# Clipped score units with a second matmul, shared rows held in SBUF, and a table added by its own load

## The chip, the cores and the metric

The kernel runs on one core of one Trainium2 chip. The metric is the device time of one execution in microseconds (us), the median over several runs. The profile is one execution taken by the hardware profiler; its times are counted from the start of its span.

## The reference

One block of a transformer over x of shape (4, 2048, 256): an attention-like layer with a triangular ("bump") kernel in place of softmax, then a mixture of experts, each with a layer norm before and after and a residual. Cut to what matters here:

```python
# attention: B=4 batches, T=2048 tokens, H=16 heads, D=16 per head; per head one projected number per token
q_proj, k_proj = q @ Wproj.T, k @ Wproj.T            # (B, T, H)
bw = softplus(log_bandwidth) + 1e-4                  # (H,)
# out_i = sum_j max(0, 1 - |q_i - k_j| / bw_h) * v_j , divided by T
ctx = bump(q_proj, k_proj, v) / T
x = x + layernorm(ctx)
# experts: 64 experts, top 8, capacity 128 per expert, groups of 2 batches of the hidden states taken together
shared = silu(xn @ Wg) * (xn @ Wu) @ Wd * sigmoid(xn @ sgate)
y = sum over the 8 experts of weight_e * expert_e(xn)   # only the first 128 tokens of an expert count
x = x + layernorm(y + shared)
```

All arithmetic is fp32. The kernel computes the bump directly: with q and k already divided by the bandwidth and k negated, a score tile is min(|q - k|, 1) - 1, which is minus the triangle, and the sum over keys is a matrix product with v.

## The kernel before

**Score units.** A unit t is one batch b, one head h and one block s of 128 keys against all 2048 queries: a 128 x 2048 tile `hat` (keys on the partitions). There are 1024 units in a fixed order (`unit`): batch, group of 8 heads, parity p of the head, key block s, and innermost j = 0 to 3, the place of the head among four. 256 units make a batch (`NU`), 128 a group (`UG`). For each t the main loop writes out by hand `score(t)`, `evict(t)`, `product(t)`, and then one step of a background queue.

- `score(t)` normally has ACT compute |q + nk| into `hat` (line 1558) and DVE take min 1 and subtract 1 (line 1562). Now and then DVE makes the absolute value itself, in two more passes (lines 1553, 1555). A running number `spare` decides: it grows by 1.9 - 1.17 with each unit on ACT and falls by what DVE does besides and by 3.6 with each unit of the DVE kind; at 1.3 or more the next unit is of that kind.
- `product(t)` issues four matmuls on PE, one for each quarter c of 512 queries, staggered: quarter c of unit t - c. The stationary operand is the head pair's 128 x 32 value tile, and the output goes to rows 32j to 32j+31 of the PSUM bank `pa` for that quarter. So the four matmuls of a step lie in four different column groups of the array. A bank accumulates over the 128 units of a group.
- `evict(t)` scales a finished bank by -1/T into SBUF (line 1572).

Score tiles, the broadcast queries `qb` and some others come from 13 buffers of 128 x 2048 (`big`); `take` pops one while the program is written, `give` returns it. Ten smaller ones (`slot`) serve the background.

**Background.** The class `Background` holds tasks with an engine, a cost in us, dependencies and buffers. In each step of the main loop it emits, in queue order, the tasks that are ready by a table of lags (`LAG`), as long as the engine's debt is under its cap (`CAP`, per step: PE 0.84, from the third batch on 0.88). So all other work (projections of the next batches, the expert layer of finished ones, the experts over batches 0 and 1) is woven into the scoring at planned places, and each engine then runs its queue in order. What is left after the last unit is written out by `drain`, which plans without scoring.

**Expert results.** Rows of batches 0 and 1 go into one table `y_d[0]`; rows of batches 2 and 3 into two tables `y_d[1]`, `y_d[2]`. `finish(b)` computes the shared expert for the four 512-token chunks of a batch (`shared(c)`) and stores the rows as the start value of the table (line 619); for batch 2 (`NE` = 2) they are also stored to `ysh_d` (line 624), for a repair path that is normally skipped. The experts' results are then added by indirect accumulating DMAs from the POOL queue (line 1066 for the first half, line 1258 for the items of the second half). For the last batch the shared rows stay in SBUF, its table rows start from zeros (`zfill`), and the final norm adds them.

**Tail.** After the last unit: the last batch's front part, its routing (a chain of max and replace on DVE), the remaining shared rows, 15 items of hot experts, and `final(c)`, the last norm of each chunk: load the table rows from the SP queue (line 1281), for batches 2 and 3 a second table too and a DVE add (line 1288), add SBUF rows if there are any (line 1314), statistics (1292), scale with a power on POOL (1298), norm on ACT (1307), and an accumulating DMA from POOL onto the output (1321). The scatters of the items depend on `stored[2]`, the stores of batch 2's shared rows.

Of the kernel before, what the change touches and what calls it, by code (L numbers as in the profile page):

```python
# [25 lines left out]
class Background:  # L26
# [6 lines left out]
    CAP = {"pe": 0.84, "dve": 0.65, "act": 0.30, "pool": 1.5, "sp": 2.0}  # L33
# [107 lines left out]
def sandwich_kernel(ctx: ExitStack, tc: tile.TileContext, x_in, wqT, bq, wkT, bk, wvT, bv, wprojT, log_bw,  # L141
# [84 lines left out]
    with ExitStack() as ph:  # L226
# [29 lines left out]

        NES, ess = 4, []
# [11 lines left out]
        def give(tag):  # L269
            bg.free["big"].append((tag, bg.t))  # L270
# [12 lines left out]
        for t_ in vst:  # L283
            nc.gpsimd.memset(t_, 0.0)

# [170 lines left out]
        def finish(b, after=()):  # L456
# [104 lines left out]
            def shared(c):  # L561
# [56 lines left out]
                free_act = a  # L618
                free_ys = bg.add("sp", 1.0, lambda ys=ys, r0=r0: nc.sync.dma_start(yrows(r0, CH, 0),
# [647 lines left out]
        def final(env, c, deps, more=None, xd=(), tag=""):  # L1267
# [14 lines left out]
            l0 = l1 = bg.add("sp", 1.0, lambda: load(0), deps, get={yy: "big" if two else "slot"}, env=env)  # L1282
            if two:
                l1 = bg.add("sp", 1.0, lambda: load(1), [l0])
# [26 lines left out]
            if two:  # L1311
                a = bg.add("dve", 1.25, add, [a])
# [41 lines left out]
        lb = small.tile([P, H], F32, name="lb")  # L1354
# [26 lines left out]
        ab = small.tile([P, H], F32, name="ab")  # L1381
        nc.scalar.activation(ab, lb, AF.Abs)
        ex = small.tile([P, H], F32, name="ex")
        nc.scalar.activation(ex, ab, AF.Exp, scale=-1.0)
        u = small.tile([P, H], F32, name="u")
        nc.vector.tensor_scalar_add(u, ex, 1.0)
        lu = small.tile([P, H], F32, name="lu")
        nc.scalar.activation(lu, u, AF.Ln)
        one = small.tile([P, H], F32, name="one")
        nc.vector.tensor_scalar(one, u, 1.0, None, ALU.is_equal)  # L1390
        nc.vector.tensor_add(lu, lu, one)
        den = small.tile([P, H], F32, name="den")
# [149 lines left out]
        spare = [0.0]  # L1542

        def score(t):
# [7 lines left out]
            if spare[0] >= 1.3:  # L1552
                nc.vector.tensor_scalar(ht, qb[n][0], k, None, ALU.add)  # L1553
                hi = ht.bitcast(I32)
                nc.vector.tensor_scalar(hi, hi, 0x7fffffff, None, ALU.bitwise_and)  # L1555
                spare[0] -= 3.6
            else:
                nc.scalar.activation(ht, qb[n][0], AF.Abs, bias=k)  # L1558
                spare[0] += 1.9 - 1.17
            if s == NT - 1:  # L1560
                give(qb.pop(n)[1])
            nc.vector.tensor_scalar(ht, ht, 1.0, 1.0, ALU.min, ALU.subtract)  # L1562
# [16 lines left out]
        def product(t):  # L1579
            for c in range(4):  # L1580
# [5 lines left out]
                if w == 0:  # L1586
                    pa[k, c] = acc.tile([P, BK], F32, tag=f"pa{c}", name=f"pa_{k}_{c}")
                nc.tensor.matmul(pa[k, c][32 * j:32 * j + 32, :],  # L1588
                                 lhsT=vt[b, s].rearrange("p a w -> p (a w)")[:, h // 2 * VW + p * D:h // 2 * VW + p * D + 32],
# [200 lines left out]
```

## Time and profile before

| what | value |
|---|---|
| median of 3 runs | 2338.87 us (2335.26 to 2339.05) |
| profiled execution | 2339.91 us, span 2338.0 us |
| mean granted TensorE clock | 0.954 |
| PE, ACT, DVE busy | 1952.5, 1966.8, 1996.1 us |
| POOL busy | 490.4 us |
| first score unit done, last one done | 67.6 us, 2034.9 us |
| DMA moved | 274.32 MB, mean 117 GB/s |

In a row of the profile, a group of instructions is named by line, engine and operation, then what it writes and reads (out<-in, buffer numbers left out) with shapes and count; after the bar come the time it was busy, the mean of one in ns, and how long the engine had been idle just before, with what ended that idle time. PE is matrix multiplication, PEld its loading of weights, DVE the vector engine, ACT the scalar engine, POOL GpSimd, SP the engine that issues most DMAs. An fp32 matmul shows as two records.

### The profile page before, as it was taken

The numbers are of one execution on the slowest core, as the hardware profiler recorded it, in microseconds if no ns is written. First come the engines' busy times: TensorE is split into PE (matmuls) and PEld (weight loads), VectorE is DVE, ScalarE is ACT, GpSimd is POOL, SyncE is SP. The second block draws the span as 40 slices with busy tenths as digits, with TensorE's granted clock in tenths as the row PEclk, the third lists the DMA queues.
The fourth block names the chain that finished last, engine by engine and source line by source line (L and its number), as shares of the span: only waits on it lengthen the run. The fifth ranks groups of instructions, "written<-read, shape, count | busy, mean of one in ns | idle before, by whom it ended". The sixth has DMA issues, their size and how long they took to land. (4 is left out here: it accounts for less than half of the span.)

```text
span 2338.0 us, 32679 instructions
## 1 busy us (share of the span) xinstructions
PE 1952.5 (84%) x12552; PEld 687.2 (29%) x12552; DVE 1996.1 (85%) x3102; ACT 1966.8 (84%) x1269; POOL 490.4 (21%) x339
## 2 busy tenths in 40 slices
PE   7898979888799899677899887878888889987783
PEld 4332323222223222112222222223332223364342
DVE  4799999898999889999989998989999979886335
ACT  2899999898999998999999998989999989742213
POOL 1001010010120000003200003446553234442463
PEclk9999999999999999989999998999999999988897
DMA  4243534427351202142302014465544243355758
GB/s 127 91 133 120 184 103 153 151 88 264 117 162 64 91 19 70 37 147 69 112 19 81 28 54 122 114 186 151 174 121 136 57 134 90 102 177 147 177 124 197
DMA packets 195078, 274.32 MB, mean 117 GB/s; under 512 B 24833, under 2 KB 165505, under 8 KB 194145
## 3 DMA queue, kind: packets, MB, share of 16 engines
q1 hardware_dynamic: 165680, 235.33, 31.2%
q0 software_dynamic: 23824, 31.70, 8.3%
q10 hardware_dynamic: 5408, 5.11, 0.7%
q8 instruction: 101, 1.65, 0.3%
q14 instruction: 65, 0.52, 0.1%
HBM read 189.18 MB, written 82.90 MB: 116 GB/s over the span
## 5 line engine op out<-in xcount | busy, mean ns | idle before, releaser
L1558 ACT ACTIVATE hat<-qb,nk 128x2048 f32<-128x2048 f32 x959 | 1837.3, 1995 | 112.8 <-DMA qb<-zq_d 57.5
L1588 PE MATMUL pa<-hat,v 128*32 128x512 f32 x8192 | 1115.3, 620 | 284.4 <-DVE hat L1562 272.3
L1562 DVE TENSOR_SCALAR hat<-hat 128x2048 f32<-128x2048 f32 x1024 | 1230.3, 1223 | 97.2 <-ACT hat L1558 91.3
L1588 PEld LDWEIGHTS pa<-hat,v 128*32 128x32 f32 x8192 | 186.2, 110 | 900.0 <-DVE hat L1562 652.6
L1066 POOL DMA_INDIRECT y_d<-s,ix x64 | 147.8, 2309 | 286.7 <-DVE s L1064 145.4
L573 PE MATMUL k<-s,sgu 128*128 128x512 f32 x352 | 198.4, 651 | 0.0
L1041 POOL DMA_INDIRECT s<-tab_d,ix x64 | 106.0, 1657 | 327.6 <-DMA qb<-zq_d 259.0
L499 POOL TENSOR_TENSOR rsc<-rsc,mhalf 128x2 f32<-128x2 f32 x24 | 53.4, 2225 | 521.2 <-DVE rsc L498 521.0
L602 PE MATMUL k<-sd,s 128*128 128x256 f32 x384 | 113.7, 428 | 16.9 <-DVE s L589 7.4
L442 PE MATMUL k<-s,s 128*32 128x512 f32 x768 | 102.4, 592 | 0.0
L602 PEld LDWEIGHTS k<-sd,s 128*128 128x128 f32 x384 | 72.2, 205 | 86.4 <-issue 47.8
L573 PEld LDWEIGHTS k<-s,sgu 128*128 128x128 f32 x352 | 54.8, 192 | 136.3 <-issue 121.2
L305 POOL TENSOR_TENSOR rsa<-rsa,mhalf 128x4 f32<-128x4 f32 x16 | 30.8, 1925 | 290.9 <-DVE rsa L304 285.6
L1553 DVE TENSOR_SCALAR hat<-qb,nk 128x2048 f32<-128x2048 f32 x65 | 83.1, 1279 | 0.1
L1555 DVE TENSOR_SCALAR hat<-hat 128x2048 int32<-128x2048 int32 x65 | 79.9, 1229 | 2.2
L350 PE MATMUL k<-h,s 128*128 128x256 f32 x256 | 73.0, 413 | 0.0
L713 DVE MAX8 codes<-scT 128x8 f32<-128x1152 f32 (+2 forms) x48 | 63.4, 1321 | 0.2
L350 PEld LDWEIGHTS k<-h,s 128*128 128x128 f32 x256 | 45.4, 195 | 54.4 <-issue 48.6
L715 DVE MATCH_REPLACE8 scT<-codes,scT 128x1152 f32<-128x1152 f32 (+2 forms) x44 | 57.6, 1310 | 0.0
L607 DVE TENSOR_SCALAR s<-k,gt 128x256 f32<-128x256 f32 x48 | 22.8, 480 | 36.5 <-PE k L602 32.0
L442 PEld LDWEIGHTS k<-s,s 128*32 128x32 f32 x768 | 31.6, 138 | 54.0 <-issue 53.2
L1258 POOL DMA_INDIRECT y_d<-v,ix x28 | 39.9, 1426 | 23.5 <-DMA y_d<-s 7.9
(319 smaller groups left out, 1643.2 us busy)
## 6 DMA issues: line engine op xcount, KB each, us to landing
qb<-zq_d SPq DMA_DIRECT2D x128, 512.0 KB, 5.5
s<-m_d SPq DMA_DIRECT2D x48, 512.0 KB, 4.8
s<-_attn_hidden_states_dram SPq DMA_DIRECT2D x28, 512.0 KB, 5.5
v_d<-h SPq DMA_DIRECT2D x48, 192.0 KB, 2.6
v<-v_d SPq DMA_DIRECT2D x48, 192.0 KB, 2.5
h<-fn_expert_gate_up_w_dram SPq DMA_DIRECT2D x32, 256.0 KB, 3.5
s<-fn_expert_gate_up_w_dram SPq DMA_DIRECT2D x32, 256.0 KB, 2.8
b<-y_d SPq DMA_DIRECT2D x16, 512.0 KB, 9.3
```

The lines of the kernel that those rows point to most:

```text
L350: nc.tensor.matmul(env[pk][:, i * F:(i + 1) * F], lhsT=xv[:, k, o:o + P], rhs=wv[:, k, :], start=(k == 0), stop=(k == KF - 1))
L442: nc.tensor.matmul(env[pz][c * CR:(c + 1) * CR, :], lhsT=xv[:, r, :], rhs=env[mp][:, k * 2 * F:(k + 1) * 2 * F], start=(r == 0 and k == 0) ...
L573: nc.tensor.matmul(env[p_], lhsT=sgu[:, k, o:o + P], rhs=featview(env[xT])[:, k, :], start=(k == 0), stop=(k == KF - 1))
L602: nc.tensor.matmul(env[py][:, i * F:(i + 1) * F], lhsT=env[acts[f // 2]][:, o:o + P], rhs=sd[:, f, :], start=(f == 0), stop=(f == NI - 1))
L713: a = bg.add("dve", 1.25, lambda c8=c8: nc.vector.max(out=c8, in_=scT[:, :w]), ev + [a])
L1041: g = bg.add("pool", 1.3, lambda: nc.gpsimd.indirect_dma_start(out=xg(), out_offset=None, in_=tab_d[half][:, :], in_offset=bass.IndirectOf ...
L1066: s = bg.add("pool", 1.9, lambda: nc.gpsimd.indirect_dma_start(out=y_d[half][:, :], out_offset=bass.IndirectOffsetOnAxis(ap=iv(), axis=0), ...
L1553: nc.vector.tensor_scalar(ht, qb[n][0], k, None, ALU.add)
L1555: nc.vector.tensor_scalar(hi, hi, 0x7fffffff, None, ALU.bitwise_and)
L1558: nc.scalar.activation(ht, qb[n][0], AF.Abs, bias=k)
L1562: nc.vector.tensor_scalar(ht, ht, 1.0, 1.0, ALU.min, ALU.subtract)
L1588: nc.tensor.matmul(pa[k, c][32 * j:32 * j + 32, :], lhsT=vt[b, s].rearrange("p a w -> p (a w)")[:, h // 2 * VW + p * D:h // 2 * VW + p * D ...
```

## The change

Three things. (1) For a chosen unit, DVE makes two tiles: `hat`, q clipped between -nk and 1-nk, and `low`, q clipped between -1-nk and -nk. Their difference is min(|q + nk|, 1) up to a constant, so PE multiplies `hat` by v and `low` by -v (`neg`, made by DVE); the constant -1 becomes minus the sum of v over the keys, which POOL adds up in `pro` and PE and DVE turn into `csum`, subtracted at the eviction. The old DVE kind stays where buffers or the place in the group don't allow this one. (2) For chunks 2 and 3 of batch 2 the shared rows stay in SBUF and the final norm adds them; they are still stored to `ysh_d`, their table rows start from zeros, and they are no longer in `stored[2]`. (3) Where a chunk has rows in SBUF to add, its second table is loaded by an accumulating DMA from POOL onto the first, in place of a load and a DVE add. Beside these, the planner's PE caps become 0.86 and 0.92, the final norm's single load is planned with a delay of 9 steps, and scratch of the prologue is moved into one tile.

```diff
-    CAP = {"pe": 0.84, "dve": 0.65, "act": 0.30, "pool": 1.5, "sp": 2.0}
+    CAP = {"pe": .86, "dve": 0.65, "act": 0.30, "pool": 1.5, "sp": 2.0}
...
+        LATE, held = (2, 3), {}
...
+        pro = small.tile([P, 12 * D + 8], F32, name="pro")
+        near = const.tile([P, 3], F32, name="near")
+        csum = const.tile([P, 1], F32, name="csum")
+        for i in range(3):
+            nc.gpsimd.memset(near[:, i:i + 1], i - 1.0)
...
+                if b == NE and c in LATE:
+                    held[c] = env, ys, yy
+                    free_ys = bg.add("sp", 1.0, lambda ys=ys, c=c: nc.sync.dma_start(rows(ysh_d, c * CT, CH),
+                                                                                    chunkview(env[ys])), yy)
+                    return
...
-            l0 = l1 = bg.add("sp", 1.0, lambda: load(0), deps, get={yy: "big" if two else "slot"}, env=env)
-            if two:
+            l0 = l1 = bg.add("sp", 1.0, lambda: load(0), deps, get={yy: "big" if two else "slot"}, env=env,
+                             lat=None if two else 9)
+            onto = two and more is not None and not tag
+            if onto:
+                l1 = bg.add("pool", 1.3, lambda: nc.gpsimd.dma_start(y3(), yrows(r0, CH, 1), accum_op=ALU.add), [l0], lat=4)
+            elif two:
                 l1 = bg.add("sp", 1.0, lambda: load(1), [l0])
...
-            if two:
+            if two and not onto:
                 a = bg.add("dve", 1.25, add, [a])
...
+        def sums():
...
+            def mm():
+                for j in range(4):
+                    nc.tensor.matmul(env["cs"][2 * D * j:2 * D * j + 2 * D, :1], lhsT=pro[:, 2 * D * j:2 * D * j + 2 * D],
+                                     rhs=near[:, 2:3], start=True, stop=True)
+            q, bg.q = bg.q, []
+            a = bg.add("pe", 0.4, mm, get={"cs": "bank"}, env=env)
+            a = bg.add("dve", 0.15, lambda: nc.vector.tensor_copy(csum, env["cs"][:, :1]), [a], put=["cs"], env=env)
+            bg.q += q
+            bg.flush([a])
...
-            if spare[0] >= 1.3:
-                nc.vector.tensor_scalar(ht, qb[n][0], k, None, ALU.add)
...
+            u = t % NU
+            if u % UG == 0:
+                nc.gpsimd.memset(pro[:, :8 * D], 0.0)
+            room = 3 + (s >= 9) + (u % UG >= UG - 24)
+            if spare[0] >= 1.3 and 4 <= u % UG < UG - 12 and len(bg.free["big"]) >= room and (True):
+
+                low[t] = take(f"low_{b}_{h}_{s}")
+                i = len(clipped) % 2
+                kk = pro[:, 12 * D + 4 * i:12 * D + 4 * i + 3]
+                neg[t] = pro[:, (8 + 2 * i) * D:(10 + 2 * i) * D]
+                tot = pro[:, 2 * D * j:2 * D * j + 2 * D]
+                nc.vector.tensor_scalar(kk, near, k, None, ALU.subtract)
+                nc.vector.tensor_scalar(neg[t], value(t), -1.0, None, ALU.mult)
+                nc.gpsimd.tensor_tensor(out=tot, in0=tot, in1=value(t), op=ALU.add)
+                nc.vector.tensor_scalar(low[t][0], qb[n][0], kk[:, 0:1], kk[:, 1:2], ALU.max, ALU.min)
+                nc.vector.tensor_scalar(ht, qb[n][0], kk[:, 1:2], kk[:, 2:3], ALU.max, ALU.min)
+                clipped.add(t)
+                spare[0] -= 2.7
+                bg.debt["pe"] += 1.1
             else:
...
-                    nc.vector.tensor_scalar(ct[b, g][0][:, c * BK:(c + 1) * BK], pa.pop((k, c)), -1.0 / T, None,
-                                            ALU.mult)
+                    nc.vector.tensor_scalar(ct[b, g][0][:, c * BK:(c + 1) * BK], pa.pop((k, c)), csum, -1.0 / T,
+                                            ALU.subtract, ALU.mult)
...
+                if tt in low:
+                    nc.tensor.matmul(pa[k, c][32 * j:32 * j + 32, :], lhsT=neg[tt], rhs=low[tt][0][:, c * BK:(c + 1) * BK],
+                                     start=False, stop=False)
+                nc.tensor.matmul(pa[k, c][32 * j:32 * j + 32, :], lhsT=value(tt), rhs=hat[tt][0][:, c * BK:(c + 1) * BK],
+                                 start=first_, stop=last_)
...
+                if u % UG == UG - 8:
+                    sums()
...
-                    bg.CAP = dict(bg.CAP, pe=0.88, dve=0.75, act=0.4)
+                    bg.CAP = dict(bg.CAP, pe=.92, dve=0.75, act=0.4)
...
-                    if l < 0:
+                    if l < 0 and c - NE * NCH in held and not tag:
+                        e_, y_, d_ = held[c - NE * NCH]
+                        f_ = final(env, c, deps, lambda e_=e_, y_=y_: e_[y_][:, :CH * F], d_)
+                        bg.add("act", 0.0, lambda: None, [f_], put=[y_], env=e_)
+                    elif l < 0:
                         final(env, c, deps, tag=tag)
```

More of the change, by code (lines that the diff above doesn't have):

```diff
@@ L1350, in norm_x0 @@
             xt0.append(done)
-        lb = small.tile([P, H], F32, name="lb")
+        lb, ab, ex, u, lu, one, den = (pro[:, i * H:(i + 1) * H] for i in range(7))
         nc.sync.dma_start(lb, log_bw.rearrange("(a h) -> a h", a=1).to_broadcast([P, H]))
@@ L1378, in sandwich_kernel @@
         nc.sync.dma_start(bvb, bv.rearrange("(a f) -> a f", a=1).to_broadcast([P, F]))
-        ab = small.tile([P, H], F32, name="ab")
         nc.scalar.activation(ab, lb, AF.Abs)
-        ex = small.tile([P, H], F32, name="ex")
         nc.scalar.activation(ex, ab, AF.Exp, scale=-1.0)
-        u = small.tile([P, H], F32, name="u")
         nc.vector.tensor_scalar_add(u, ex, 1.0)
-        lu = small.tile([P, H], F32, name="lu")
         nc.scalar.activation(lu, u, AF.Ln)
-        one = small.tile([P, H], F32, name="one")
         nc.vector.tensor_scalar(one, u, 1.0, None, ALU.is_equal)
         nc.vector.tensor_add(lu, lu, one)
-        den = small.tile([P, H], F32, name="den")
         nc.vector.tensor_scalar_sub(den, u, 1.0)
@@ L1542, in sandwich_kernel, with value @@
         spare = [0.0]
+        low, neg, clipped = {}, {}, set()
+        def value(t):
+            b, g, p, s, j, h = unit(t)
+            o = h // 2 * VW + p * D
+            return vt[b, s].rearrange("p a w -> p (a w)")[:, o:o + 2 * D]
+        def sums():
+            env = {}
+            def mm():
[7 more added lines that the diff above has]
+            bg.flush([a])
         def score(t):
@@ L1551, in score @@
             k = nks[b][:, c:c + 1]
-            if spare[0] >= 1.3:
[L1553 to L1556, printed above, removed]
-            else:
-                nc.scalar.activation(ht, qb[n][0], AF.Abs, bias=k)
-                spare[0] += 1.9 - 1.17
+            u = t % NU
[16 more added lines that the diff above has]
+                bg.debt["pe"] += 1.1
+            else:
+                if spare[0] >= 1.3:
+                    nc.vector.tensor_scalar(ht, qb[n][0], k, None, ALU.add)
+                    hi = ht.bitcast(I32)
+                    nc.vector.tensor_scalar(hi, hi, 0x7fffffff, None, ALU.bitwise_and)
+                    spare[0] -= 3.6
+                else:
+                    nc.scalar.activation(ht, qb[n][0], AF.Abs, bias=k)
+                    spare[0] += 1.9 - 1.17
+                nc.vector.tensor_scalar(ht, ht, 1.0, 1.0, ALU.min, ALU.subtract)
             if s == NT - 1:
                 give(qb.pop(n)[1])
-            nc.vector.tensor_scalar(ht, ht, 1.0, 1.0, ALU.min, ALU.subtract)
         def evict(t):
@@ L1587, in product @@
                     pa[k, c] = acc.tile([P, BK], F32, tag=f"pa{c}", name=f"pa_{k}_{c}")
-                nc.tensor.matmul(pa[k, c][32 * j:32 * j + 32, :],
-                                 lhsT=vt[b, s].rearrange("p a w -> p (a w)")[:, h // 2 * VW + p * D:h // 2 * VW + p * D + 32],
-                                 rhs=hat[tt][0][:, c * BK:(c + 1) * BK],
-                                 start=(p == 0 and s == 0), stop=(p == 1 and s == NT - 1))
+                first_, last_ = p == 0 and s == 0, p == 1 and s == NT - 1
+                if tt in low:
[3 more added lines that the diff above has]
+                                 start=first_, stop=last_)
             if 3 <= t < B * NU + 3:
                 give(hat.pop(t - 3)[1])
+                if t - 3 in low:
+                    give(low.pop(t - 3)[1])
         nks, last, mst = {0: nk0}, {}, []
@@ L1651, in sandwich_kernel @@
                     nc.gpsimd.memset(zt_[:, :CH * F], 0.0)
-                    zfill = [(1, c) for c in range(NE * NCH, B * NCH)] + [(0, c) for c in range((B - 1) * NCH, B * NCH)]
+                    zfill = [(1, c) for c in range(NE * NCH, B * NCH)] + [(0, c) for c in [NE * NCH + i for i in LATE] + list(range((B - 1) * NCH, B * NCH))]
                 if b == 1 and u % 8 == 4 and zfill:
```

## The prediction

> **What bounds the kernel now.** I read the page first: sections 1 and 5 for the engines and the costliest groups.
>
> ```profile
> PE 1952.5 (84%) x12552; PEld 687.2 (29%) x12552; DVE 1996.1 (85%) x3102; ACT 1966.8 (84%) x1269; POOL 490.4 (21%) x339
> L1558 ACT ACTIVATE hat<-qb,nk 128x2048 f32<-128x2048 f32 x959 | 1837.3, 1995 | 112.8 <-DMA qb<-zq_d 57.5
> L1588 PE MATMUL pa<-hat,v 128*32 128x512 f32 x8192 | 1115.3, 620 | 284.4 <-DVE hat L1562 272.3
> L1562 DVE TENSOR_SCALAR hat<-hat 128x2048 f32<-128x2048 f32 x1024 | 1230.3, 1223 | 97.2 <-ACT hat L1558 91.3
> L1553 DVE TENSOR_SCALAR hat<-qb,nk 128x2048 f32<-128x2048 f32 x65 | 83.1, 1279 | 0.1
> L1555 DVE TENSOR_SCALAR hat<-hat 128x2048 int32<-128x2048 int32 x65 | 79.9, 1229 | 2.2
> ```
>
> Nearly all time goes to 1024 score units: 959 cost ACT 1.995 us and DVE 1.223; 65 cost DVE 1.279 + 1.229 + 1.223 = 3.73 us and ACT nothing. Three engines are almost equally busy, so a mean doesn't say which has room. I therefore cut the scoring stretch at every 64th end of L1562 and asked for busy time by stage (columns: PE, PEld, DVE, ACT, POOL, clock, DMA, GB/s):
>
> ```profile
> 67.60:187.40 119.80, 106.12 (x862) 39.42 (x862) 108.97 (x130) 112.49 (x60) 5.61 (x3) 0.99 0.36 117
> 419.50:541.20 121.70, 100.32 (x742) 31.67 (x738) 111.20 (x152) 111.09 (x58) 10.37 (x5) 0.97 0.41 135
> 789.90:913.70 123.80, 117.65 (x648) 32.74 (x648) 114.27 (x115) 116.66 (x68) 0.00 (x0) 0.99 0.17 57
> 1912.60:2034.90 122.30, 112.36 (x707) 38.45 (x708) 106.19 (x119) 109.82 (x72) 47.20 (x24) 0.97 0.41 108
> 67.60:2035.00 1967.40, 1685.59 (x11331) 525.53 (x11331) 1797.94 (x2415) 1869.27 (x1081) 356.49 (x195) 0.97 0.36 110
> 2034.90:2338.00 303.10, 218.79 (x855) 131.85 (x852) 168.69 (x586) 81.54 (x164) 124.65 (x110) 0.85 0.66 160
> ```
>
> Scoring lasts 1967.4 us. ACT is idle for 98 of them (5%) and DVE for 169; they set the pace. PE is idle for 282 us, but unevenly: in the third block shown it is busy 95%. The wait view (100 to 2030 us) says that PE already holds ACT up, through score buffers it has not yet freed:
>
> ```profile
> ACT hat L1558 <- PE pa L1588: 49.6, 52, 3.1
> ```
>
> How PE does a product is read from the timeline where it had seven steps queued:
>
> ```profile
> 999.77 3.18 PE L1588 MATMUL pa<-hat,v 128*32 128x512 f32 x28
> ```
>
> A 128x512 matmul is two records. A step's four matmuls sit in four different 32-column groups (32j), and 28 records took 3.18 us: seven rounds of four at once. The last lasts 0.59, so a round is (3.18 - 0.59)/6 = 0.43 us and a step, two rounds, 0.86.
>
> **Part 1, clipped units.** The order of instructions gives 61 clipped units, 17 of the old DVE kind, 946 on ACT.
>
> ACT: 13 units fewer x 1.995 = -26 us.
>
> DVE, per clipped unit: two full passes with two pointer scalars each. One pointer costs 1.279 - 1.223 = 0.056 more than none, so two cost 1.34. Does the fast rate survive two pointers? The nearest row is
>
> ```profile
> L309 DVE TENSOR_SCALAR s<-s,mva,rsa 128x256 f32<-128x256 f32 x48 | 17.5, 406 | 0.0
> ```
>
> 256 elements with two pointers. Taking the 2048-element pass as 0.156 fixed + 1.067 streamed, the fast rate gives 0.156 + 0.112 + 0.133 = 0.40, half that rate 0.53; 0.406 says fast. The small ones (128x3, 128x32) are bounded by 0.16 and 0.22 (rows of 4 and 64 elements); I take 0.35 for both. 61 x 3.03 + 17 x 3.73 + 946 x 1.223 = 1405 against 65 x 3.73 + 959 x 1.223 = 1415: -10. The eight copies of the column sums each stand right behind a step's product on PE, so DVE may wait about 1 us there: +8, beside PE's delay below. DVE stays about where it was.
>
> PE: each clipped unit adds four matmuls, 244 in all, one in each of four steps, **in the same column group** as the main one it precedes. The price is bounded below by a quarter of a step, 0.86/4 = 0.215 (if it packed beside the others), above by its own two rounds, 0.86. The row shows overlap among four different groups only. The Trainium skill, "TensorE: Matmul & The Clock Gate", Part 3 (packing small matmuls), speaks against the change: tiles overlap because they occupy different positions of the array, and "MATMULs are pc-monotone in start AND end — strict FIFO, no reordering". So nothing behind the extra one overtakes it. The rule's sum is 244 x 0.86 = +209 us of PE; packing would make it +52. I take 0.86. The change itself books only 1.1 us per unit; background matmuls, weighed by columns, stay at 539 us before and 537 after, merely shifted between blocks.
>
> Now block by block. Allowed time = the block's time less 2.0 us for each ACT unit fewer; PE need = its busy time + 0.86 x extra matmuls + shifted background. 0 to 63: 28 extra, 106.1 + 24.0 - 2.6 = 127.5 against 119.8 - 4 = 115.8: PE binds, +7.7 on 119.8. 192: 32 extra, 100.3 + 27.5 - 2.4 = 125.4 on 121.7: +3.7. 384: 25 extra, 117.7 + 21.4 - 5.1 = 134.0 on 123.8: +10.2. 960: 24 extra, 112.4 + 20.6 - 0.3 = 132.7 on 122.3: +10.4. Likewise +2.6, +2.7 and +6.5 at 64, 128 and 256. Of the other nine, PE fits in eight: two get two ACT units more each (+4, +4), two get fewer (-2, -4), four get the same; at 576 PE needs 132.4 of 133.8 (-1.4). They sum to +0.6. Together **+44 us**, where the ACT count alone promised -26. That fills PE to 100%; at 97% it is +76. PE's busy time, though, includes drains between switches of shape (28 queued records overlap them), which pulls back; I keep 44.
>
> POOL: 61 adds of 128x32 and eight fills. The skill, "SBUF — State Buffer", "Who interferes with whom", says that a DVE instruction in a two-port mode and a GpSimd one exclude each other, whichever started first holding the port. Were each add to block DVE for about 0.6 us, that were +37. But POOL's arithmetic beside DVE is what stretches here (L499, 2.23 us in scoring; L1298, 1.59 in the last 65 us), while L1562 stays at 1.22 whether or not a POOL operation runs; I take 0. What queues behind the adds are expert gathers and scatters, and PE's column sum waits for the last add; the adds end 12 units before a group does, the sum stands 8 before, and POOL is 18% busy: nothing.
>
> The prologue's scratch moving into one tile: same instructions in the first 60 us, 0.
>
> **Parts 2 and 3, the tail (303 us).** PE is busy for 219, and these waits bind:
>
> ```profile
> 2178.76 2.93 PE L602 MATMUL k<-sd,s 128*128 128x256 f32 x6 [4.51 <-ACT s L587]
> 2187.05 1.41 DVE L1292 BATCH_NORM_STATS2 v<-s 128x6 f32<-128x256 f32 x4 [7.35 <-DMA s<-y_d]
> 2189.10 2.93 PE L602 MATMUL k<-sd,s 128*128 128x256 f32 x6 [7.41 <-DVE s L589]
> 2204.55 1.65 POOL L1258 DMA_INDIRECT y_d<-v,ix  x1 [7.89 <-DMA y_d<-s]
> ```
>
> DVE stands at a final norm's load with L589 behind it, so PE starves; the first item's scatter waits for the third batch's last shared rows. The change plans final-norm loads of the first half with nine steps' delay, and the scatters no longer wait for those rows. I book PE's 4.5 + 7.4 = -12. What is late next are gathers that wait for scatters to free "v" buffers (PE waits 11 us at L1223); I book none of that. Two row buffers stay held to the end, so five of eight early final stores move behind item scatters on POOL; PE's own queue covers that. SP loses two row stores of 0.5 MB and six final loads and gains two zero stores in the second batch, where DMA is 0.2 to 0.3 busy: 0.
>
> The last stage: six table loads (0.5 MB) move from SP to POOL as accumulating DMAs. DVE loses six adds and gains two: -4 x 1.23 = -4.9. POOL gains 6 x 1.32 issue time, each behind its plain load's landing (median 9.3 us); behind four of them queue the second chunk's power and the first store. From 2265 us on:
>
> ```profile
> q0 software_dynamic: 4668, 4.55, 44.3%
> q1 hardware_dynamic: 8448, 8.39, 37.0%
> ```
>
> Per MB the POOL queue, accumulating mostly, takes 9.7% of 73 us, the other 4.4%: 0.52 MB moved costs 2.0 us more of all engines, six of them +12, while DMA is 0.86 to 1.16 busy. Bounds -5 to +15; I take +5. Tail: **-7**.
>
> Sum against the profiled execution (span 2338.0, its own time 2339.9, which is 1.0 above the median 2338.87 and 0.9 above the highest run): +44 - 7 = +37, so 2376 from the median.
>
> **Rivals.**
> (B) *The extra matmul packs* at 0.215 to 0.43 us because other groups run beside it: PE needs 52 to 105 us of its 282, the blocks give -26 to -20, with the tail 2306 to 2312. For: a step already shows four at once. Against: same group, order kept. It decides below about 0.64 us per extra matmul, where scoring's +7 and the tail's -7 cancel. This is the side on which it gets faster.
> (C) *The last stage queues behind POOL*: powers and stores wait behind accumulating loads, +15 there instead of +5; on top of part 1, 2386. For: DMA is full there. Against: DVE's chain shortens.
> (D) *PE loses less than it seems*: lags between clipped units (five to eight apart) are absorbed by score buffers and shorter drains, part 1 comes to about +7, and with -7 it ends near 2339.
> That the change doesn't do what it says is partly so: 17 units keep the old way where buffers lack.
>
> **How the numbers follow.** Forecast with (C): 0.68, slower; B 0.25; D 0.07. What a measurement here can tell from no change is about 0.2%, 4.7 us. The range reaches down to B's 2304 (packing with a slightly better tail) and up to PE at 97%, 2338.9 + 76 - 7 = 2408. The likeliest case alone spans 2352 to 2408.
>
> **What would show it.** Right: the extra line's matmuls with starts 0.43 apart and alone; PE over 95% busy in blocks 0, 256, 384, 960; ACT's waits for PE well over 49.6 us; ACT busy 26 us less with scoring longer; first item scatter earlier than 170 us after scoring; no 7 us wait of DVE at L1292. Wrong: scoring under 1967 us with ACT still 95% busy; or extra matmuls starting beside three others.

## The result, and the profile after

The changed kernel takes 2462.55 us (median of 4 runs, 2460.57 to 2464.21) against 2338.96 us (four runs of the kernel before, one more than above): a ratio of 1.0528, 95% interval 1.0510 to 1.0547, so 124 us slower. The forecast was 37 us slower, with a range that ended at 2408. From the page of the changed kernel, the engines and the groups of the score units (busy, mean ns of one, idle before and what ended it):

```profile
PE 2138.7 (87%) x13104; PEld 759.8 (31%) x13104; DVE 1983.2 (81%) x3193; ACT 1950.0 (79%) x1254; POOL 531.9 (22%) x417
L1610 ACT ACTIVATE hat<-qb,nk 128x2048 f32<-128x2048 f32 x946 | 1820.9, 1995 | 247.3 <-PE pa L1644 140.9
L1644 PE MATMUL pa<-hat,v 128*32 128x512 f32 x8192 | 1307.9, 616 | 215.6 <-DVE hat L1612 204.2
L1642 PE MATMUL pa<-low,pro 128*32 128x512 f32 x488 | 254.5, 603 | 4.8 <-DVE low L1598 4.5
L1598 DVE TENSOR_SCALAR low<-qb,pro 128x2048 f32<-128x2048 f32 x61 | 83.2, 1363 | 8.0 <-PE pa L1644 5.9
L1599 DVE TENSOR_SCALAR hat<-qb,pro 128x2048 f32<-128x2048 f32 x61 | 81.9, 1342 | 0.0
```

The main matmul is now line 1644 and the extra one line 1642 (488 records, 244 matmuls); ACT's unit is line 1610 and DVE's min pass line 1612. ACT does 13 units fewer, as counted. But ACT's busy share has fallen from 84 to 79%, DVE's from 85 to 81%, and PE's has risen from 84 to 87%. What grew is ACT's waiting, most of it for PE.

By stage, cut as before at every 64th finished unit (columns: PE, PEld, DVE, ACT, POOL busy, clock, DMA share, GB/s); shown are blocks 0, 192, 384, 704 and 960, then all of scoring and what is left after it:

```profile
67.60:201.40 133.80, 128.37 (x902) 46.76 (x902) 103.51 (x126) 107.75 (x56) 6.84 (x6) 0.98 0.28 93
450.40:580.80 130.40, 121.47 (x881) 40.98 (x877) 105.48 (x139) 107.27 (x56) 12.78 (x11) 0.99 0.37 114
842.90:979.90 137.00, 128.67 (x687) 36.14 (x686) 109.36 (x165) 118.14 (x70) 3.70 (x10) 1.00 0.16 50
1494.60:1626.00 131.40, 112.14 (x699) 34.89 (x699) 103.19 (x135) 108.66 (x66) 48.54 (x27) 0.95 0.38 102
2022.70:2158.10 135.40, 131.97 (x778) 45.09 (x770) 106.20 (x131) 112.10 (x73) 49.26 (x29) 1.00 0.36 93
67.60:2158.10 2090.50, 1864.52 (x11865) 593.49 (x11865) 1788.02 (x2506) 1854.92 (x1067) 383.56 (x257) 0.98 0.35 103
2158.10:2462.40 304.30, 224.41 (x869) 135.45 (x869) 165.50 (x586) 78.77 (x163) 138.12 (x120) 0.85 0.70 159
```

Scoring is 123 us longer (2090.5 against 1967.4) and the tail is where it was (304.3 against 303.1), so the whole loss lies in scoring. PE's busy time there grew by 179 us, and its idle time shrank only from 282 to 226. The granted clock (0.98 there against 0.97) is not the reason. Nowhere is PE busy 100% of a block: in the four fullest it is 94 to 97.5% (128.37 of 133.8 is 96%). And blocks became longer in which PE had room. The first two lines are blocks 448 and 704 before (the forecast's block boundaries lie a unit later), the third is block 448 after:

```profile
911.20:1028.90 117.70, 82.23 (x548) 18.25 (x547) 111.82 (x107) 114.47 (x62) 0.00 (x0) 0.93 0.19 56
1408.00:1529.70 121.70, 96.66 (x656) 30.51 (x656) 105.93 (x119) 109.25 (x68) 52.91 (x25) 0.93 0.46 124
979.90:1110.40 130.50, 114.79 (x650) 31.05 (x648) 117.16 (x125) 122.17 (x68) 0.20 (x1) 0.96 0.20 61
```

Block 448 is 12.8 us longer with PE busy for 88% of it (7 of them also without the extra matmuls, in `skip_extra` below), block 704 9.7 us longer with PE busy for 85%.

ACT's waits for score buffers that PE still holds grew from 49.6 us to the sum of these two rows of the waits (us in all, times, longest):

```profile
ACT hat L1610 <- PE pa L1644: 140.9, 109, 4.9
ACT hat L1610 <- PE pa L1642: 16.0, 11, 3.5
```

DVE, too, now stands behind PE, at results of background matmuls. In the forecast these had no row of their own; over the whole of scoring the waits of DVE for PE's "k" banks add up to 68.5 us before and 135.0 after. The largest after (the first four of these places had 12.0, 17.9, 11.0 and 3.2 us before):

```profile
DVE s L1067 <- PE k L1060: 26.8, 18, 5.1
DVE s L615 <- PE k L610: 24.4, 13, 4.3
DVE s L1077 <- PE k L1074: 23.2, 22, 3.7
DVE s L1470 <- PE k L1461: 19.1, 10, 3.9
DVE csum L1572 <- PE k L1568: 13.4, 8, 3.6
```

What an extra matmul costs PE is seen in the timeline of PE at one clipped unit (start, length of the group, records; a matmul is two records, so the lines at 986.65 and 987.11 are one extra matmul):

```profile
986.13 0.59 PE L581 MATMUL k<-s,sgu 128*128 128x512 f32 x1
986.65 0.62 PE L1642 MATMUL pa<-low,pro 128*32 128x512 f32 x1
986.67 0.63 PE L1644 MATMUL pa<-hat,v 128*32 128x512 f32 x3
987.11 0.59 PE L1642 MATMUL pa<-low,pro 128*32 128x512 f32 x1
987.12 1.47 PE L1644 MATMUL pa<-hat,v 128*32 128x512 f32 x7
988.39 0.59 PE L1642 MATMUL pa<-low,pro 128*32 128x512 f32 x1
988.40 0.64 PE L1644 MATMUL pa<-hat,v 128*32 128x512 f32 x3
```

The next step's extra matmul starts 1.74 us after this one (988.39 - 986.65): four rounds of 0.43, where a step without an extra one has two. So it costs 0.86 us here, where PE is behind, as forecast. But it is not alone. Three main matmuls start 20 ns behind it. In program order the extra one is the first of its step, what ran before it was background (L581), and the first main matmul behind it has its column group. So these three are taken to be the other three main matmuls of the step, which overtook. The trace doesn't name the column group; the experiment `spread_groups` tests this reading.

A rival would be that the queue holds another order than the program text. Clipped units whose hat pass came late speak against it:

```profile
1514.26 1.34 DVE L1599 TENSOR_SCALAR hat<-qb,pro 128x2048 f32<-128x2048 f32 x1
1514.40 1.04 PE L1642 MATMUL pa<-low,pro 128*32 128x512 f32 x2 [0.51 <-DVE low L1598]
1515.65 1.06 PE L1644 MATMUL pa<-hat,v 128*32 128x512 f32 x8 [0.21 <-DVE hat L1599]
```

Here the extra matmul runs alone, and all eight main records start after the hat pass has ended at 1515.60, although three of the four main matmuls read tiles that were ready before. In 26 of the 61 clipped units the hat pass ended 0.24 to 1.29 us after the extra matmul's start, and in none of the 26 did a main matmul start before that end. So the first main matmul does stand ahead of the other three. While it waits for its tile, they wait behind it; where its tile is ready and only its column group is taken, they pass.

### The profile page after: what moved, and what is told of

The parts are those of the page before. It is cut to its first block, busy times and chain, and to the rows that moved or that the text cites. A ratio compares the mean times of both kernels' runs of the same rounds, so it can differ in the third digit from the quotient of the medians.

```text
span 2462.4 us, 33985 instructions
## 1 busy us (share of the span) xinstructions
PE 2138.7 (87%) x13104; PEld 759.8 (31%) x13104; DVE 1983.2 (81%) x3193; ACT 1950.0 (79%) x1254; POOL 531.9 (22%) x417
## 3 DMA queue, kind: packets, MB, share of 16 engines
q8 instruction: 105, 1.72, 0.3%
## 5 line engine op out<-in xcount | busy, mean ns | idle before, releaser
L1610 ACT ACTIVATE hat<-qb,nk 128x2048 f32<-128x2048 f32 x946 | 1820.9, 1995 | 247.3 <-PE pa L1644 140.9
L1644 PE MATMUL pa<-hat,v 128*32 128x512 f32 x8192 | 1307.9, 616 | 215.6 <-DVE hat L1612 204.2
L1612 DVE TENSOR_SCALAR hat<-hat 128x2048 f32<-128x2048 f32 x963 | 1162.3, 1223 | 157.7 <-ACT hat L1610 153.8
L1644 PEld LDWEIGHTS pa<-hat,v 128*32 128x32 f32 x8192 | 239.8, 109 | 885.1 <-DVE hat L1612 529.6
L1642 PE MATMUL pa<-low,pro 128*32 128x512 f32 x488 | 254.5, 603 | 4.8 <-DVE low L1598 4.5
L581 PE MATMUL k<-s,sgu 128*128 128x512 f32 x352 | 196.5, 645 | 0.0
L450 PE MATMUL k<-s,s 128*32 128x512 f32 x768 | 164.1, 598 | 0.0
L610 PE MATMUL k<-sd,s 128*128 128x256 f32 x336 | 96.7, 415 | 9.7 <-DVE s L615 9.5
L581 PEld LDWEIGHTS k<-s,sgu 128*128 128x128 f32 x352 | 54.6, 190 | 132.3 <-issue 121.9
L1598 DVE TENSOR_SCALAR low<-qb,pro 128x2048 f32<-128x2048 f32 x61 | 83.2, 1363 | 8.0 <-PE pa L1644 5.9
L1599 DVE TENSOR_SCALAR hat<-qb,pro 128x2048 f32<-128x2048 f32 x61 | 81.9, 1342 | 0.0
L1642 PEld LDWEIGHTS pa<-low,pro 128*32 128x32 f32 x488 | 42.6, 109 | 75.0 <-issue 51.9
L450 PEld LDWEIGHTS k<-s,s 128*32 128x32 f32 x768 | 50.0, 140 | 50.8 <-issue 48.6
```

The source lines that it names most:

```text
L450: nc.tensor.matmul(env[pz][c * CR:(c + 1) * CR, :], lhsT=xv[:, r, :], rhs=env[mp][:, k * 2 * F:(k + 1) * 2 * F], start=(r == 0 and k == 0) ...
L581: nc.tensor.matmul(env[p_], lhsT=sgu[:, k, o:o + P], rhs=featview(env[xT])[:, k, :], start=(k == 0), stop=(k == KF - 1))
L610: nc.tensor.matmul(env[py][:, i * F:(i + 1) * F], lhsT=env[acts[f // 2]][:, o:o + P], rhs=sd[:, f, :], start=(f == 0), stop=(f == NI - 1))
L1598: nc.vector.tensor_scalar(low[t][0], qb[n][0], kk[:, 0:1], kk[:, 1:2], ALU.max, ALU.min)
L1599: nc.vector.tensor_scalar(ht, qb[n][0], kk[:, 1:2], kk[:, 2:3], ALU.max, ALU.min)
L1642: nc.tensor.matmul(pa[k, c][32 * j:32 * j + 32, :], lhsT=neg[tt], rhs=low[tt][0][:, c * BK:(c + 1) * BK], start=False, stop=False)
```

## Experiments

Theory P: the loss is PE's extra time. Rival Q: it is the second buffer and DVE's bursts. Rival R: it is the rest of the change (sums, planner, tail). All times are medians; ratios are to the kernel before timed beside it, whose median lay between 2334 and 2339 us. `skip_extra`, `half_extra` and `spread_groups` keep the planner's order of instructions, so they differ from the change in the extra matmuls alone; the other runs move background work as well.

**1. Leave the extra matmul out (`skip_extra`).**

```
-                if tt in low:
+                if False:
                     nc.tensor.matmul(pa[k, c][32 * j:32 * j + 32, :], lhsT=neg[tt], rhs=low[tt][0][...
```

> The changed kernel, but the extra matmul of each clipped unit (neg x low) is left out: 244 matmuls fewer, everything else kept, the second score buffer, its two VectorE passes, the planner's 1.1 us per clipped unit and the tail; that product is missing from the output. Theory P (TensorE's extra time is the loss): 244 x 0.86 = 209 us of matmul time go, ScalarE still has 13 units fewer, so it ends at 2300 to 2330 us. Rival Q (the loss comes from the second buffer and the bursts of VectorE work, three microseconds at a stretch, with ScalarE waiting behind them): it stays above 2420 us.

Measured: 2351.62 us, ratio 1.0055 (1.0037 to 1.0074). DVE's bursts stay, and 111 us go, so they are not the loss. The second buffer is still taken, but PE no longer reads it, so that half of Q is left to run 3. But it is not the 2300 to 2330 of theory P either: something else still costs. The loss in block 704 goes too:

```profile
1414.80:1534.70 119.90, 94.27 (x651) 28.75 (x651) 102.82 (x135) 107.91 (x66) 47.32 (x27) 0.93 0.41 112
67.60:2051.00 1983.40, 1690.68 (x11377) 520.23 (x11377) 1782.25 (x2505) 1847.03 (x1067) 383.66 (x257) 0.97 0.36 109
```

Here block 704 has 25.6 us of idle PE. The 24 extra matmuls of the changed kernel added 17.9 us of PE's busy time to it (112.14 - 94.27), which would have fitted, and still the block became 11.5 us longer.

**2. Half the price (`half_extra`).**

```
-  nc.tensor.matmul(pa[k, c][32*j:32*j+32, :], lhsT=neg[tt], rhs=low[tt][0][:, c*BK:(c+1)*BK], ...)
+  nc.tensor.matmul(pa[k, c][32*j:32*j+32, :BK//2], lhsT=neg[tt], rhs=low[tt][0][:, c*BK:c*BK+BK//2], ...)
```

> The changed kernel, but each extra matmul takes 256 of its 512 columns, so about half the price, near 0.43 us; half of that product is missing from the output. Theory P1 (each extra microsecond of TensorE lengthens scoring in proportion, whatever the block's mean load): halfway between the changed kernel and the one without the matmul, 2380 to 2400 us. Theory P2 (the forecast's rule: only blocks in which TensorE's need passes the block's time pay, the rest is absorbed): at half price nearly all blocks fit, so 2310 to 2330 us, as good as without. Rival Q: above 2420 us.

Measured: 2392.61 us, 1.0238 (1.0221 to 1.0255); P1's range, and 60 us above P2's. This is the run that judges the forecast's rule. By that rule the half price (0.43 x the extra matmuls on top of each block of `skip_extra`, over the block's length) lengthens only blocks 0 and 960, by 2.3 and 2.1 us. It cost 41. The first half of the price costs 41 us and the second 70, so it does get dearer as PE fills, but it is never free.

```profile
67.60:2083.10 2015.50, 1762.32 (x11864) 586.24 (x11863) 1785.80 (x2505) 1849.38 (x1067) 382.19 (x257) 0.98 0.35 107
```

**3. No second buffer (`no_low_buffer`).**

```
-  low[t] = take(f"low_{b}_{h}_{s}")
+  low[t] = hat[t]
```

> The changed kernel with the same instructions, but the low pass writes the buffer that the hat pass then overwrites, and the extra matmul reads that one: no second 1 MB score buffer is held by a clipped unit, so ScalarE can run further ahead; the product of the extra matmul is another one than asked. Theory P: 2450 to 2465 us, nothing gained or at most 10 us. Rival B (the second buffer takes ScalarE's lead, and that is why it waits for TensorE): under 2420 us.

Measured: 2453.24 us, 1.0497 (1.0474 to 1.0521): 9 us of 124 by the medians, 7 by the ratios, whose intervals overlap. So the buffer counts for little, and Q is out. (The run isn't clean: the extra matmul now waits for the hat pass too, and PE's idle time before it grows from 4.8 to 30.5 us.)

**4. No unit clipped (`no_clip`), the same with the old planner shares, and the tail parts alone.**

```
-  if spare[0] >= 1.3 and ... and (True):
+  if spare[0] >= 1.3 and ... and (False):
```

> The changed kernel with no unit clipped: the units that VectorE takes are all of the old kind (add, and, min), the rest of the change stays (column sums and their copies, fills, the planner's new shares of 0.86 and 0.92, both tail parts). Theory P: all of the 124 us goes, 2330 to 2345 us. Rival R (column sums, new planner shares or the tail parts carry a part of the loss): over 2350 us.

Measured: 2355.06 us, 1.0083 (1.0058 to 1.0108). So about 17 us are not due to clipping, which is rival R's part. Three more runs took it apart.

```
old_shares:          -  CAP pe .86, from the third batch on .92
                     +  CAP pe .84, from the third batch on .88
no_clip_old_shares:  both edits
tail_only:           both edits, and
                     -  if u % UG == UG - 8: sums()
                     -  nc.gpsimd.memset(pro[:, :8 * D], 0.0)      # at each group's first unit
                     +  nc.gpsimd.memset(csum, 0.0)                # once
```

> The changed kernel with the planner's shares of TensorE as before (0.84, 0.88 instead of 0.86, 0.92). If the new shares cause the 16 us that the kernel without clipped units still loses: 2440 to 2450 us. If they do not: 2458 to 2466 us.

Measured: the whole change with the old shares (0.84, 0.88) takes 2462.35 us, 1.0534 (1.0505 to 1.0563). The shares are not it.

> The changed kernel with no unit clipped and the planner's shares as before; column sums, their copies and fills and both tail parts stay. If the shares cause the 16 us of the kernel without clipped units: 2330 to 2342 us. If the column sums (14 us of VectorE waiting for TensorE) cause it: 2348 to 2358 us.

Measured: 2356.95 us, 1.0094 (1.0068 to 1.0120). The shares are not it here either.

> The two tail parts alone on the kernel before: no unit clipped, no column sums, no fills, old shares. By the forecast's working -7 us: 2332 us. If the tail parts gain nothing, as the changed kernel's last stretch of 304 us against 303 suggests: 2336 to 2342 us. If they carry the 16 us of the kernel without clipped units, for instance through row buffers held to the end: 2348 to 2358 us.

Measured: 2338.39 us, 1.0011 (1.0000 to 1.0021). What is left between the last two is the column sums with their fills: 18.6 us with the old shares (2356.95 - 2338.39).

**5. The sums' copy issued later (`no_clip_late_copy`).** In `no_clip`, DVE's row for the copy in the waits of scoring is

```profile
DVE csum L1572 <- PE k L1568: 16.0, 8, 3.0
```

so each of the eight copies waits 2 us for PE.

```
-  bg.flush([a])        # matmul, and the copy right behind it
+  bg.flush([m_])       # the matmul; the copy follows three units later
```

> The changed kernel with no unit clipped, and VectorE's copy of the column sums issued three units after their matmul instead of right behind it. If the 17 us that the sums cost (2355 against 2338 without them) are VectorE waiting for TensorE's column sum (16 us in the waits): 2338 to 2344 us. If they are the fills, the bank that is taken or the order of the background: 2350 to 2358 us.

Measured: 2345.85 us (20 runs), 1.0037 (1.0025 to 1.0050). The wait is gone: in the answer for this line, with us and times,

```profile
  PE k L1568: 0.9, 2
```

and 9 us with it. That is about half of the cost; the other half (7 us against the tail parts alone) was not settled between the fills, the bank and the background's shifted order. The run fell between its two expectations.

**6. The four extra matmuls in four column groups (`spread_groups`).**

```
-  nc.tensor.matmul(pa[k, c][32 * j:32 * j + 32, :], lhsT=neg[tt], ...
+  nc.tensor.matmul(pa[k, c][32 * ((j + c) % 4):32 * ((j + c) % 4) + 32, :], lhsT=neg[tt], ...
```

> The changed kernel, but the four extra matmuls of a clipped unit go to four different 32-column groups (group j + c instead of j for the quarter c); instructions, operand sizes and order stay, the extra products are added to other output rows. Theory G (each column group has a queue of its own, so an extra matmul costs a full 0.86 us only because all four stand in one group): the four steps hold five matmuls per group, the price falls to 0.22 to 0.43 us each, 2375 to 2405 us, near the kernel with half-width extra matmuls (2393). Rival S (strictly in order: an extra matmul holds up whatever stands behind it): 2450 us and over.

Measured: 2420.11 us, 1.0358 (1.0331 to 1.0385): 42 us less, with nothing changed but output rows. So the price hangs on the column group, as G says. (Strict order is not ruled out by this run: under it, too, matmuls of different groups could run side by side. Against it speaks the timeline above.) The gain is smaller than G said; the time lies between the ranges of G and S:

```profile
67.60:2112.30 2044.70, 1811.48 (x11865) 600.07 (x11863) 1785.90 (x2505) 1851.85 (x1067) 382.13 (x257) 0.98 0.34 105
```

PE's busy time over `skip_extra` is 120.8 us, 0.50 per extra matmul, against 0.71 in the changed kernel (173.8 of 244) and 0.29 at half width. (Why busy time counts less than the 0.86 that the starts show was not taken apart.) Much of the price stays: of 161 pairs of following extra matmuls less than 3 us apart, 29 start less than 1.6 us apart, of 171 such pairs in the changed kernel none.

**7. Book the true price (`honest_debt`).**

```
-  bg.debt["pe"] += 1.1
+  bg.debt["pe"] += 3.4
```

> The changed kernel with one number changed: the planner books 3.4 us of TensorE for a clipped unit (four extra matmuls at 0.86) where it booked 1.1, so that background matmuls keep clear of the extra ones. Theory P1 (TensorE is late where extra matmuls and background fall together, and the in-order queues of VectorE and ScalarE hand that lateness on): scoring gets shorter than the changed kernel's 2090 us by 20 to 50 us, while background that no longer fits moves behind scoring and lengthens the last stretch beyond 304 us; in all 2420 to 2450. Rival P3 (only the amount of TensorE work counts, not where it lies): 2458 to 2470 us, what scoring gains the end loses.

Measured: 2781.75 us, 1.1910 (1.1878 to 1.1941), a miss for both theories, and more than one thing had changed. `spare` counts DVE's background work; with less of that emitted, more units were clipped (101 in place of 61), each of which pushed more background out. The stretch behind scoring grew from 304 to 719 us. So the units were fixed by a list, and the booking changed both ways.

```
-  if spare[0] >= 1.3 and 4 <= u % UG < UG - 12 and ...:
+  if t in PIN:                                  # the changed kernel's 61 units
-  if spare[0] >= 1.3:
+  if t in OLD:                                  # its 17 of the old kind
-  bg.debt["pe"] += 1.1
+  bg.debt["pe"] += 3.4                          # same_units_34;  0.0 in same_units_0
```

> The changed kernel with its 61 clipped and 17 old VectorE units fixed by a list, so that their number cannot grow, and the planner booking 3.4 us of TensorE per clipped unit instead of 1.1. Theory P1 (TensorE's lateness where extra matmuls and background fall together is handed on by the in-order queues): scoring 30 to 70 us shorter than the changed kernel's 2090, the stretch behind it longer by 40 to 140 us (61 x 2.3 = 140 us of background matmul time booked elsewhere). Total by P1 with a stretch behind that absorbs half: 2440 to 2480 us; by rival P3 (only the amount of TensorE work counts): 2460 to 2600 us with scoring shorter by no more than the background that has left it.

Measured: 2486.90 us, 1.0637 (1.0602 to 1.0671). Scoring, then the stretch behind it:

```profile
67.60:2107.70 2040.10, 1828.84 (x11640) 571.12 (x11639) 1773.56 (x2451) 1844.80 (x1048) 308.53 (x221) 0.98 0.32 99
2107.70:2486.50 378.80, 265.38 (x1093) 168.38 (x1093) 183.85 (x640) 86.30 (x184) 182.00 (x156) 0.82 0.69 161
```

Scoring is 50 us shorter (P1's range; PE is busy 36 us less there, so P3 would allow no more than 36), the stretch behind it 74 us longer. The total is above P1's range and inside P3's: what leaves scoring costs more behind it.

> The same fixed list, with nothing booked for a clipped unit: background stays where the planner puts it without clipped units, so it falls together with the extra matmuls. If the booking of 1.1 us protects scoring: scoring longer than 2090 us by 10 to 30, the stretch behind 2 to 10 us shorter, total 2465 to 2485 us. If the booking only moves work about: 2450 to 2465 us.

Measured: 2491.19 us, 1.0662 (1.0630 to 1.0695): scoring 31 us longer (2121.0), the stretch behind 7 us shorter. Without a booking the same units take 29 us longer than the change, more than expected.

**8. Is ACT's saving worth anything? (`clip_free`, `clip_free_11`).** The extra matmul and the second buffer left out, the copy late, the units fixed; in the first with no booking, in the second with the 1.1 put back. That is the only difference:

```
-  bg.debt["pe"] += 0.0
+  bg.debt["pe"] += 1.1
```

> The same fixed list with everything taken away that the earlier runs priced: the extra matmuls are left out (their product is missing from the output), no second score buffer, the column-sum copy three units late, nothing booked. What stays of clipping is ScalarE's 13 units fewer and VectorE's passes. If ScalarE's 26 us are worth their full size once nothing else is late: 2345.9 (the late copy without clipped units) - 26 = 2320 us. If the pace is set by all three engines' order and not by ScalarE's load: 2335 to 2346 us.

Measured: 2379.36 us, 1.0182 (1.0147 to 1.0217): both expectations missed, on the slow side.

> The last kernel (extra matmuls left out, no second buffer, late copy, fixed list of clipped units) with the booking of 1.1 us per clipped unit put back, so that background work stands again where it stood when that list was made. If what matters is where VectorE's clipped passes fall among its background work: 2333 to 2345 us (the kernel without extra matmuls, 2351.6, less what the late copy and the buffer gave, 9 each at most). If the late copy or the fixed list itself made the 28 us: 2370 to 2385 us.

Measured: 2323.52 us, 0.9956 (0.9942 to 0.9971). One line each, first without and then with the booking:

```profile
67.60:2069.50 2001.90, 1691.32 (x11373) 523.66 (x11373) 1789.22 (x2506) 1846.73 (x1066) 390.00 (x256) 0.97 0.36 108
```

```profile
67.60:2020.20 1952.60, 1671.85 (x11358) 518.89 (x11357) 1781.51 (x2501) 1843.30 (x1064) 378.36 (x253) 0.98 0.36 110
```

The same units, the same instructions in the whole program, ACT time in scoring within 3.5 us and DVE time within 8, and yet 49 us of scoring between them: only the place of the background differs. The better of the two is 22 us under `no_clip_late_copy` (2345.85), or 19 by the ratios. That is near the 26 of the sum, but as placing alone moves 49 to 56 us, it can't be put down to ACT's units. As the run leaves out the product, it is only an example of what clipping could bring here if PE's part were free.

**9. The two tail parts one by one (`late_only`, `onto_only`).** Both start from `tail_only`. `onto_only` also leaves out the zero rows of the second part and the nine-step delay, which `late_only` keeps.

```
late_only:  -  onto = two and more is not None and not tag
            +  onto = False
onto_only:  -  if b == NE and c in LATE:
            +  if False:
```

> The kernel before with the second part alone: the third batch's late shared rows stay in SBUF for the final norm, no clipped units, no sums, no accumulating table loads. By the forecast's working (TensorE's waits of 4.5 and 7.4 us vanish): 2336 - 12 = 2324 us. If another wait takes their place, as the whole tail's +1 to 2 us suggests: 2331 to 2339 us.

Measured: 2331.28 us, 0.9984 (0.9971 to 0.9998): about 4 us gained by the ratio, 6 by the medians, a third to a half of what was forecast. The kernel before with this part alone beats both kernels, by little.

> The kernel before with the third part alone: the second table of the last batch's final norm is added during its load (four accumulating loads instead of loads and adds). By the forecast's working +5 (bounds -5 to +15): 2341 us. If the DMA queues have room for it and VectorE's four adds go: 2331 to 2336 us.

Measured: 2345.89 us (20 runs), 1.0034 (1.0024 to 1.0045): 8 us lost, 5 forecast. What is late is seen on POOL in the last stretch (the profiled execution was the longest of the 20, 2352.4 us):

```profile
2317.96 1.32 POOL L1300 DMA_DIRECT2D b<-y_d  x1 [12.71 <-SPq L1788]
2318.76 1.84 POOL L1339 DMA_DIRECT2D out_dram<-b  x1
2319.55 2.12 POOL L1316 TENSOR_TENSOR v<-v,mhalf 128x4 f32<-128x4 f32 x1
```

and in DVE's waits from the end of scoring on:

```profile
DVE v L1319 <- POOL v L1316: 25.8, 10, 12.5
```

The same wait before, then in the changed kernel:

```profile
DVE v L1301 <- POOL v L1298: 10.1, 10, 1.8
DVE v L1318 <- POOL v L1315: 6.9, 7, 1.1
```

The fourth accumulating load (L1300) keeps POOL idle for 12.7 us. (The row names SP's line 1788, which waits for the same semaphore; in the program L1300 waits for its plain load, the last that SP issues, at 2306.69.) A power (L1316) queues behind it, and DVE waits for that power: 25.8 us, where the kernel before has 10.1. This is rival C's mechanism. In the changed kernel it isn't seen: with both tail parts together DVE waits 6.9 us there.

## Why the prediction was wrong, step by step

One table puts the runs in order of ACT's waits, over scoring, for score buffers that PE holds:

| kernel | ACT's wait for PE, us | scoring, us | time, us |
|---|---|---|---|
| late copy, no unit clipped | 48.6 | 1977.8 | 2345.9 |
| before | 49.6 | 1967.4 | 2338.9 |
| no extra matmul, no buffer, late copy, booked | 53.1 | 1952.6 | 2323.5 |
| no unit clipped | 69.6 | 1987.4 | 2355.1 |
| no extra matmul | 80.1 | 1983.4 | 2351.6 |
| no extra matmul, no buffer, late copy, not booked | 96.0 | 2001.9 | 2379.4 |
| half extra matmuls | 109.4 | 2015.5 | 2392.6 |
| spread over the groups | 118.0 | 2044.7 | 2420.1 |
| the change's units, 3.4 booked | 133.9 | 2040.1 | 2486.9 |
| no second buffer | 139.1 | 2076.2 | 2453.2 |
| the change | 156.9 | 2090.5 | 2462.6 |
| the change's units, nothing booked | 198.5 | 2121.0 | 2491.2 |

From before to the change the wait grows by 107 us and scoring by 123. From 80 us on the waits and scoring rise together but for one neighbouring pair; below, the order is rough. The two go together; no run took the waits away and left the extra matmuls in.

- *Where PE binds, a block lengthens by what exceeds it; elsewhere nothing (+44).* This step failed, and carries the error: the extra matmuls cost 111 us, because PE's idle time in a block was not a reserve. From before to the change, column sums included, the seven blocks that were to bind lengthened by 79 us in place of 44, and the nine others, which were to come to +0.6 together, by 44. Against `skip_extra`, where only the extra matmuls differ, it is 80 and 27. `half_extra` shows it with nothing else changed: an addition that by the rule lengthens two blocks, by 4 us together, cost 41. At full price, the same rule on the blocks of `skip_extra` gives 56 us at 100% and 87 at 97%; measured were 111. My 97% case (+76 for all of part 1, against about 122) was the better one and still too low. The reading that the waits support is that three engines, 86 to 95% busy in scoring before, run their queues in order with little lead. An extra burst of PE makes ACT wait for a buffer and DVE for a bank, and most of what they lose there isn't made up later. That is argued from the waits; no run tested it alone. That the place of work counts, and not only its amount, is shown by kernels with the same units: scoring differs by 49 us within experiment 8, which has no extra matmuls, and by 31 between the change and `same_units_0`, which have them.
- *Price of an extra matmul, 0.86 us.* Right: starts of extra steps are 1.74 and 1.72 us apart, against 0.86 for a plain step. (The forecast's row of 28 records is three and a half steps of eight records, not seven steps; its seven rounds and the 0.86 stand.) The reason given was wrong, so that the price came out is in part luck. I wrote that nothing behind it overtakes, and named extra matmuls starting beside three others as a sign against me. They do start so, and the price is still two rounds, since it is the one column group that carries two matmuls per step. Spreading the groups took 42 us off. Rival B's overlap therefore exists across groups and was worth nothing in the group the change uses.
- *ACT -26.* ACT has 13 units fewer, but the busy time of its units fell by 16 us (1837.3 to 1820.9), not 26: in the records following units overlap, by a little less after the change (1.916 us of busy time per unit before, 1.925 after, at a mean length of 1.995). Without the extra matmuls the units gave 3.5 us (2355.06 - 2351.62), which is within the intervals. The step "2.0 us of block per unit" was not confirmed: the 22 us of `clip_free_11` may be placing.
- *DVE.* Right in size: the low and hat passes took 1.363 and 1.342 us, 1.34 forecast; the two small ones 0.40 together, 0.35 forecast. Column sums: +8 booked, about 17 measured (2355.06 - 2338.39, with the new shares), of which about 9 went with the wait. The wait itself was 1.7 to 2 us per copy, not 1.
- *POOL adds, 0.* No harm is seen: 21 of the min passes overlap an add and take 1.239 us on average, the others 1.223.
- *Tail -7.* Measured +1 to +2 (0 to 5 by the interval of `tail_only`), in parts -4 and +8 against -12 and +5. The first item scatter came at 2302.77, 145 us after scoring in place of 170, and DVE's 7 us wait before the statistics of a final norm is gone (1.4 us in all there), as forecast. The replacement that I did not price is in the waits of the changed kernel's tail:

```profile
PE k L610 <- DVE s L615: 9.5, 2, 8.9
PE pa L610 <- DVE s L615: 7.8, 2, 7.2
```

  In the same stretch DVE, at L615, waits 11.2 us for final stores to leave their row buffers. I had named the buffers and the stores that move behind the scatters, and written that PE's queue covers them. PE waits there instead. `late_only`, without the accumulating loads, has waits of 7.6 and 7.0 us at the same place, so they come with the second part; that the held buffers cause them was not tried alone. PE's largest wait in this stretch after the change, 14.5 us in four times for DVE in the expert layer (L944 for L936), was not followed up.
- *Rivals.* B (2306 to 2312) and D (near 2339) are out, as the extra matmuls alone cost 111 us. C's mechanism shows where the third part stands alone, at 8 us, and not in the change.

The measured terms add up: tail +1.5, column sums +17, clipping without its matmuls -3.5, extra matmuls +111, together 126 of 124 us. The last three are differences along one chain of runs and add up by themselves; they show where the loss sits.

## What to carry to other kernels

Where several engines are nearly full and feed one another through in-order queues with a few buffers, don't count the idle time of one as room. Here, at 86 to 95%, added matmuls cost 57 to 64% of the busy time they added (41 us for 72, 111 for 174), though the smaller dose fitted nearly every block. Price such an addition first by the waits that already cross the engines, and try it at half its size before believing a load sum. A choice made from one planner's placing belongs to that placing: here, with one booking changed, the same instructions took some 55 us more.

## What the runs showed of the hardware

Matmuls of different 32-column groups can pass one another in PE's queue: three that stand behind an extra one and the next of its group started 20 ns after it, while that next one followed two rounds later, and moving the extra matmuls to other groups saved 42 us. A matmul that still waits for its tile is not passed: in 26 cases, none of those behind it started. The Trainium skill, "TensorE: Matmul & The Clock Gate", Part 3, on which the forecast leaned, says strict FIFO; within a group the starts agree with that, across groups they do not. The groups themselves are read from the program, since the trace does not show them.
